# Causal mask products of the maxima stage, moved from 64x128 halves of TensorE's array to 64x64 quarters

## The chip, the cores and the metric

The kernel runs on one core of a Trainium2 chip. TensorE (PE), VectorE (DVE), ScalarE (ACT), GpSimd (POOL) and SyncE (SP) work beside each other, each through its own list of instructions in order; TensorE multiplies with an array of 128 rows by 128 columns and writes to the accumulation memory, PSUM. The metric is the device time of one execution in microseconds; profiled times of single instructions are in us or ns as marked.

## What is computed

The reference is a network of two layers on x of 2 x 1024 x 256. Each layer adds an attention and a feed-forward part, both computed from the same normalised x. The change is in layer 0's attention, which is causal, with 32 query heads and 8 key heads of 8 values each:

```python
scores = jnp.einsum('bhqd,bhkd->bhqk', q, k_rep) / scale
qpos = jnp.arange(T)[:, None]
kpos = jnp.arange(T)[None, :]
scores = jnp.where((kpos > qpos)[None, None], -jnp.inf, scores)
attn = jax.nn.softmax(scores, axis=-1)
out = jnp.einsum('bhqk,bhkd->bhqd', attn, v_rep)
```

Layer 0's feed-forward part works with values rounded to 8 bits; layer 1 has an attention without a mask and a feed-forward part with ternary weights.

## The kernel before

Layer 0's attention goes over 16 blocks of 128 queries: b is the batch, i the block in it, in the order (0, 0) to (0, 7) and then (1, 7) to (1, 0). Of each block the kernel first finds every row's maximum per head, and later computes the scores again, turned, with the maximum already taken off.

**The maxima.** `max_units` cuts a block into units, each a call of `max_unit`. A unit computes scores of 128 queries against some keys for a pair of head groups, e = 0 and 1. The values of e = 0 lie on rows 0 to 63 of the array and those of e = 1 on rows 64 to 127, so each score product (L958) uses 64 rows and all 128 columns, and the two halves write two PSUM buffers. Then VectorE reduces each buffer to the negated maxima (`tensor_reduce`, L970). The pool `ps_s` has three such buffers, of which a unit takes two. Blocks with i > 3 have 16 units over the first 512 keys without a mask. Every block has units over the keys that reach the diagonal, of width (i % 4 + 1) x 128: four heads to a unit with width 128, two with 256, one with 384 or 512.

**The mask** is added by TensorE, in `add_mask` (product at L930), because the last 128 keys of such a unit lie on the diagonal. `mask_q` holds, for query 64t + p of a block in row 64e + p, -1e30 at the keys after it and 0 elsewhere; `ident_h` holds the identity's rows 64t to 64t + 63, once in each half of the rows. Their product for t puts the mask onto the queries 64t to 64t + 63 and adds 0 to the other 64 queries. For t = 1 only the keys 64 to 127 are touched, as no query of the second half has a masked key before. One call is four products: t = 0 and 1, for e = 0 and 1. There are 208 calls and so 832 products: four per block of width 128 (before the scores, for four heads at once, 512 columns), sixteen per block of the other widths (after each score pair, 128 columns for t = 0 and 64 for t = 1). With width 256 a unit has two such calls.

**The weights and the rest.** `weigh` computes the turned scores: two pairs of products (L1022), one of 64 and one of 35 rows on each half, all 128 columns. ScalarE takes the exponential (L1032); GpSimd zeroes what is masked in blocks on the diagonal (L1036). `gather` multiplies by v: four products over 128 rows by 9 columns, each on its own column group, in two passes (L1052). `normalise` (L1067), `turn_rows` (L1083) and `output` (L1091) finish a block. Pieces of layer 0's feed-forward part (`gu`, L288, and `f0o`, L248, over the whole array), the normalisation and the weights of layer 1 stand between.

**The order.** TensorE's order is written by hand: `one_slot` runs one step, in which `advance` issues units of maxima as a credit allows, so that they spread over the steps of the blocks before; then comes a piece of other work, then the gathering and the weights of the block in hand. The other engines' order is set by the layer that records the program. The maxima of a block must be done before its weights start, by `LEAD` or `SHORT` steps.

Of the kernel before, what the change touches and what calls it, by code (L numbers as in the profile page):

```python
# [33 lines left out]
HALF = 64  # L34
# [14 lines left out]
def two_layers(ctx: ExitStack, tc: tile.TileContext, a: dict, out: bass.AP):  # L49
# [24 lines left out]
    for name, op, fill, sign in (  # L74
# [5 lines left out]
        for e in range(2):  # L80
            for t in range(2):
                part = m[HALF * e : HALF * e + HALF, t, :]
                nc.gpsimd.affine_select(
                    out=part,
# [7 lines left out]
    ident_h, mask_q = both.values()  # L92
# [645 lines left out]
    def attention0(w, qlast, tables):  # L738
# [11 lines left out]
        with ExitStack() as es:  # L750
# [171 lines left out]
            def add_mask(out, start, stop):  # L922


                for t in range(2):
                    lo = HALF * t
                    for e in range(2):
                        rows = slice(HALF * e, HALF * e + HALF)
                        rhs = mask_q[rows, t, None, lo:]
                        nc.tensor.matmul(  # L930
                            out[e][:, :, lo:],
                            ident_h[rows, t, :],
                            rhs.to_broadcast([HALF, out[e].shape[1], P - lo]),
                            start=start and t == 0,
                            stop=stop and t == 1,
                        )

            def wait_busy(n):
# [7 lines left out]
            def max_unit(b, i, pairs, lo, width, part, masked):  # L946
# [6 lines left out]
                if four:  # L953
                    add_mask([x.rearrange("p (h k) -> p h k", h=4) for x in sc], True, False)
                for s, p in enumerate(pairs):
                    for e in range(2):
                        rows = slice(HALF * e, HALF * e + HALF)
                        nc.tensor.matmul(  # L958
                            sc[e][:, s * width : (s + 1) * width],
                            qst[b, i][0][rows, p, :],  # L960
                            kst[b][0][rows, lo // 512, p // 4, 0:width],
                            start=not four,
                            stop=s == n - 1 if four else not masked,
                        )
                    if masked and not four:
                        end = (s + 1) * width
                        add_mask([x[:, None, end - P : end] for x in sc], False, True)
# [421 lines left out]
```

## Time and profile before

| what | value |
|---|---|
| time, median of 3 runs | 1179.34 us (1178.61 to 1179.58) |
| the profiled execution's own time | 1180.16 us |
| its span, first to last instruction | 1178.4 us |
| mean granted TensorE clock | 0.936 |
| L930 mask products | 832, 75.2 us busy, mean 221 ns |
| L930 weight loads | 832, 45.2 us busy, mean 97 ns |
| L970 reductions | 608, 372.8 us busy, mean 654 ns |
| L958 score products of the maxima | 768, 94.8 + 83.4 us busy |
| L1052 gathering | 1152 passes, 171.1 us busy |

Busy times of TensorE are unions of instructions that overlap: a product's duration holds its way through the array, so that the start of the next tells more of what it costs. PEld is the weight load, which runs beside PE. In a timeline, equal instructions that follow each other on an engine are merged into one row with a count; a bracket behind a row gives the idle time before it and what ended it. The chain of work that ended last is followed back from the last instruction: at each step to what released it, or to the instruction before it on its engine.

### The profile page before, as it was taken

How to read it: one execution, taken by the hardware profiler on the slowest of the kernel's cores; microseconds unless marked ns; L12 is line 12 of the kernel's file. 1: busy time of each engine (PE TensorE's matmuls, PEld its weight loads, DVE VectorE, ACT ScalarE, POOL GpSimd, SP SyncE). 2: the span in 40 equal slices, each digit the busy share in tenths (PEclk: the TensorE clock that was granted, in tenths of full speed). 3: DMA queues.
4: the chain of work that ended last, by engine and by line, in shares of the span. 5: the costliest groups of instructions: out<-in, count | busy, mean ns of one | idle time of the engine just before them, and what ended most of it. 6: DMA issues, size and time to landing. Idle time of an engine off the chain costs nothing.

```text
span 1178.4 us, 19285 instructions
## 1 busy us (share of the span) xinstructions
PE 1039.2 (88%) x7446; PEld 497.8 (42%) x7462; DVE 764.8 (65%) x1448; ACT 545.2 (46%) x983; POOL 345.4 (29%) x394
## 2 busy tenths in 40 slices
PE   5758787897988989897989998989999999999998
PEld 2333331231432222232323333334566676676676
DVE  7467988889688997789896899334333433433331
ACT  2004461673456757586767777742232322322221
POOL 2007233324235121412223335564222312312200
PEclk9758896998899989998999999999899999999989
DMA  5342101101102010100000110019431431421200
GB/s 173 112 110 73 48 3 38 21 21 45 49 5 50 1 27 10 41 5 8 21 19 10 27 28 3 5 19 132 62 52 28 80 65 30 86 51 28 38 19 19
DMA packets 65859, 48.99 MB, mean 42 GB/s; under 512 B 20840, under 2 KB 59368, under 8 KB 65768
## 3 DMA queue, kind: packets, MB, share of 16 engines
q1 hardware_dynamic: 60568, 39.05, 15.4%
q0 software_dynamic: 4112, 8.26, 2.9%
q8 instruction: 58, 0.95, 0.3%
q10 hardware_dynamic: 1088, 0.46, 0.1%
q14 instruction: 33, 0.27, 0.1%
HBM read 34.12 MB, written 15.20 MB: 42 GB/s over the span
## 4 chain that ended last, share of the span: by engine, by line
PE 55%; DVE 27%; DMA 7%; ACT 4%; POOL 3%; issue 2%; SPq 1%; DVEq 0%; ACTq 0%; POOLq 0%
DVE mx L970 14%; PE f1gu L632 8%; PE acc L1052 8%; PE s L1022 6%; PE f1o L667 5%; PE m L958 3%; PE sk L524 3%; PE sq L489 3%; PE gu L288 2%; DMA qscr<-ptq 2%; PE pqk L440 2%; ACT p L1032 2%; PE m L930 1%; DMA qkv<-all 1%; SPq L882 1%
## 5 line engine op out<-in xcount | busy, mean ns | idle before, releaser
L970 DVE TENSOR_REDUCE mx<-m 128x1 f32<-128x512 f32 (+3 forms) x608 | 372.8, 654 | 91.4 <-PE m L958 55.2
L1032 ACT ACTIVATE p<-s 128x512 f32<-128x512 f32 x576 | 307.0, 604 | 133.7 <-PE s L1022 131.2
L1052 PE MATMUL acc<-p,v 128*9 128x512 f32 x1152 | 171.1, 613 | 2.4 <-ACT p L1032 1.2
L958 PE MATMUL m<-k,qmain 64*128 64x512 bf16 (+3 forms) x384 | 94.8, 357 | 50.5 <-DVE mx L970 39.2
L1036 POOL TENSOR_SCALAR_AFFINE_SELECT p<-p 128x512 f32<-128x512 f32 x128 | 84.8, 685 | 162.2 <-ACT p L1032 161.9
L632 PE MATMUL f1gu<-xnT,wgu 128*128 128x512 f32 x256 | 117.6, 603 | 3.1 <-DVE wgu L1294 3.1
L958 PE MATMUL m<-kmain,qmain 64*128 64x512 bf16 (+3 forms) x384 | 83.4, 333 | 24.9 <-DVE mx L970 23.0
L958 PEld LDWEIGHTS <-qmain 64*128 64x128 bf16 x768 | 50.3, 99 | 80.4 <-issue 51.2
L930 PEld LDWEIGHTS <-ident_h 64*128 64x128 bf16 x832 | 45.2, 97 | 88.1 <-issue 65.3
L646 POOL TENSOR_TENSOR sq<-h 128x512 f32<-128x512 f32 x28 | 29.2, 1041 | 180.0 <-DVE h L642 180.0
L930 PE MATMUL m<-mask_q,ident_h 64*128 64x128 bf16 (+3 forms) x832 | 75.2, 221 | 2.4 <-DVE mx L970 2.3
L1022 PE MATMUL s<-qmain,k 64*128 64x512 bf16 x288 | 67.8, 393 | 9.0 <-ACT ob L258 3.1
L632 PEld LDWEIGHTS f1gu<-xnT,wgu 128*128 128x128 f32 x256 | 47.5, 195 | 51.8 <-issue 47.8
L1022 PE MATMUL s<-qmain,kmain 64*128 64x512 bf16 x288 | 64.0, 389 | 4.9 <-ACT p L1032 2.3
L1022 PE MATMUL s<-qlast,k 35*128 35x512 bf16 x288 | 64.0, 390 | 0.0
L641 DVE SCALAR_TENSOR_TENSOR h<-h,f1gu 128x512 f32<-128x512 f32 x32 | 22.0, 687 | 64.5 <-ACT h L640 64.5
L1022 PEld LDWEIGHTS <-k 64*128 64x128 bf16 (+1 forms) x576 | 21.1, 95 | 97.9 <-issue 89.8
L497 DVE TENSOR_REDUCE m<-sq 128x16 f32<-128x2048 f32 x16 | 36.7, 2292 | 39.6 <-PE sq L489 38.9
L1022 PE MATMUL s<-qlast,klast 35*128 35x512 bf16 x288 | 61.1, 386 | 0.0
L667 PE MATMUL f1o<-k,h 128*128 128x256 f32 x256 | 59.4, 388 | 0.5 <-DVE on L557 0.5
L667 PEld LDWEIGHTS f1o<-k,h 128*128 128x128 f32 x256 | 48.9, 193 | 9.0 <-issue 1.7
L640 ACT ACTIVATE h<-f1gu 128x512 f32<-128x512 f32 x32 | 19.1, 597 | 65.7 <-PE f1gu L632 65.6
(274 smaller groups left out, 1597.6 us busy)
## 6 DMA issues: line engine op xcount, KB each, us to landing
qmain<-qscr SPq DMA_DIRECT2D x64, 96.0 KB
qkv<-all SPq DMA_DIRECT2D x16, 384.0 KB
qscr<-ptq POOLq DMA_DIRECT2D x6, 384.0 KB, 4.1
x<-in_x SPq DMA_DIRECT2D x16, 128.0 KB
qmain<-qscr SPq DMA_DIRECT2D x32, 64.0 KB
qs<-qkv SPq DMA_DIRECT2D x16, 128.0 KB
ks<-qkv SPq DMA_DIRECT2D x16, 128.0 KB
vs<-qkv SPq DMA_DIRECT2D x16, 128.0 KB
```

The lines of the kernel that those rows point to most:

```text
L489: nc.tensor.matmul(ps[:, s, r, :], columns(q, slice(S * s, S * s + HD + 8), 4 * b + r), columns(k, slice(S * s, S * s + HD + 8), 4 * b + r ...
L497: nc.vector.tensor_reduce(m, ps, AX.X, ALU.max, negate=True)
L524: nc.tensor.matmul(ps[:, s, r, :], columns(k, slice(S * s, S * s + HD + 9), 4 * b + r), columns(q, slice(S * s, S * s + HD + 9), 4 * b + r ...
L632: nc.tensor.matmul(ps[g], wgu[:, k, g * HID + hc * P : g * HID + (hc + 1) * P], xnT[n][:, k, :], start=(k == 0), stop=(k == 1),)
L667: nc.tensor.matmul(po, hs[hc // 2][:, hc % 2, i * P : (i + 1) * P], wp[:, hc, :], start=(hc == 0), stop=(hc == NHC - 1),)
L930: nc.tensor.matmul(out[e][:, :, lo:], ident_h[rows, t, :], rhs.to_broadcast([HALF, out[e].shape[1], P - lo]), start=start and t == 0, stop ...
L958: nc.tensor.matmul(sc[e][:, s * width : (s + 1) * width], qst[b, i][0][rows, p, :], kst[b][0][rows, lo // 512, p // 4, 0:width], start=not ...
L970: reduced = nc.vector.tensor_reduce(mx[b, i][:, part, e, pairs[0] : pairs[0] + n], sc[e][:, : n * width].rearrange("p (s k) -> p s k", s=n ...
L1022: nc.tensor.matmul(sc[e], kst[b][n][rows, j // 4, u, j % 4 * P : (j % 4 + 1) * P], qst[b, i][n][rows, 4 * u : 4 * u + 4, :], start=n == 0, ...
L1032: nc.scalar.activation(p, sc[e], AF.Exp, scale=scale)
L1036: nc.gpsimd.affine_select(out=by_head, in_=by_head, compare_op=ALU.is_ge, fill=0.0, base=0, pattern=[[0, 4], [1, P]], channel_multiplier=-1,)
L1052: nc.tensor.matmul(acc[32 * s : 32 * s + HD0 + 1, :], vst[b][:, j, 4 * G + s, :], ps[s], start=(j == 0), stop=(j == i),)
```

## The change

Each of the four mask products now uses 64 columns of the array instead of 128: the product for t takes from `ident_h` only the columns of its own 64 queries and writes only those 64 partitions of PSUM. It no longer adds 0 to the other half of the queries. Where the masks come first in their buffer (width 128), the product for t = 1 now begins its own accumulation and covers all 128 keys of each head, 512 columns instead of 256, because nothing else has written its half before. Elsewhere the columns that stream, 128 and 64, are as before. The number of products and loads, their order on TensorE, and everything else in the source are the same; lines below move down by two.

```diff
             def add_mask(out, start, stop):
 
 
+
                 for t in range(2):
-                    lo = HALF * t
+                    lo = 0 if start else HALF * t
+                    queries = slice(HALF * t, HALF * t + HALF)
                     for e in range(2):
                         rows = slice(HALF * e, HALF * e + HALF)
                         rhs = mask_q[rows, t, None, lo:]
                         nc.tensor.matmul(
-                            out[e][:, :, lo:],
-                            ident_h[rows, t, :],
+                            out[e][queries, :, lo:],
+                            ident_h[rows, t, queries],
                             rhs.to_broadcast([HALF, out[e].shape[1], P - lo]),
-                            start=start and t == 0,
-                            stop=stop and t == 1,
+                            start=start,
+                            stop=stop,
                         )
```

## The prediction

> **What bounds the kernel now.** I read the page's busy shares first, then the waits between 79 and 746 us, the stretch in which nearly all mask products stand (rows run from 44.3 to 745.1 us; those before 79 us belong to blocks that wait for their query loads). Columns of the waits: us in total, times, longest.
>
> ```profile
> PE 1039.2 (88%) x7446; PEld 497.8 (42%) x7462; DVE 764.8 (65%) x1448; ACT 545.2 (46%) x983; POOL 345.4 (29%) x394
> ```
> ```profile
> PE m L958 <- DVE mx L970: 55.8, 88, 4.6
> ...
> DVE mx L970 <- PE m L958: 44.6, 40, 3.2
> DVE mx L970 <- PE m L930: 28.6, 36, 3.3
> ```
>
> Neither engine bounds this stretch alone. PE waits 55.8 us for VectorE to free a score buffer, and VectorE waits 44.6 + 28.6 us for PE to fill one. With three buffers and two to a unit, each holds the other up in turn. So I followed the chain of work that ended last through the stretch and asked, for each of the 208 calls of add_mask, on whose part of the chain it falls: 21 calls lie before 79 us, where the chain is loads; of the other 187, 99 lie on PE, 76 on VectorE (five of these are shared with idle issue time or ScalarE), 12 on ScalarE or GpSimd.
>
> **The price of one division of the array.** The timeline of PE gives it. Columns: start, duration, engine, line, operation, operands with rows*columns of the array, count. Durations contain some 0.16 us of pipeline, so I read from start to start.
>
> ```profile
> 203.07 0.39 PE L1022 MATMUL s<-qmain,k 64*128 64x512 bf16 x2
> 203.30 0.38 PE L1022 MATMUL s<-qlast,k 35*128 35x512 bf16 x2
> 203.52 0.38 PE L958 MATMUL m<-k,qmain 64*128 64x512 bf16 x2
> 203.83 1.04 PE L288 MATMUL gu<-xq,wg 128*128 128x512 bf16 x4
> 204.80 1.05 PE L1052 MATMUL acc<-p,v 128*9 128x512 f32 x8
> ```
>
> From 203.30 to 203.52 a pair of products of 512 columns takes 0.216 us (the two halves of the rows run beside each other; 512 columns at 2.4 per ns). From 203.52 to 203.83 the same pair takes 0.31 us, because a product over all 128 rows follows: 0.095 us in which nothing streams. The four gu products should take 4 x 0.216 = 0.864 us and take 0.97: again 0.1 us, and here the rows stay at 128 and only the columns change, from 128 to 9. Wherever the division changes at full clock, some 500 places, the loss is about 0.09 to 0.10 us; I take 0.095. The weight loads do not matter to it: it is the same before L1067, whose loads last 0.142 us, as before L1052 with 0.088.
>
> **What the change does to one call.** Now a call shares the division 64*128 with the score products around it:
>
> ```profile
> 583.29 0.27 PE L958 MATMUL m<-kmain,qmain 64*128 64x256 bf16 x2
> 583.40 0.25 PE L930 MATMUL m<-mask_q,ident_h 64*128 64x128 bf16 x4
> 583.48 0.27 PE L958 MATMUL m<-kmain,qmain 64*128 64x256 bf16 x2
> 583.59 0.25 PE L930 MATMUL m<-mask_q,ident_h 64*128 64x128 bf16 x4
> 583.77 1.50 PE L1052 MATMUL acc<-p,v 128*9 128x512 f32 x8
> ```
>
> The score pair of 256 columns takes 0.11, the call 0.08 (128 + 64 columns, one pair after the other), and where the gathering follows, 0.18, the loss included. After the change the four products lie on four quarters and should stream together: 128 columns, 0.055 us, so **0.027 us saved** per call. That four products on the same rows do stream together is seen in the gathering, whose four, on four column groups, start within 0.02 us of each other. In the 16 calls of width 128 the sum 512 + 256 columns becomes 512: 0.107 saved. Together 192 x 0.027 + 16 x 0.107 = 6.9 us.
>
> **What it adds** is a division on either side, 64*64, that nothing else uses. The order of PE's instructions is unchanged, so I can count: 207 of the 208 calls follow a score product in 64*128 and one follows products over the whole array, which change the division already. After the call, 67 go on with L958 and 47 with L1022, both 64*128, so that 114 need a second new change; the other 94 are followed by work that changes it anyway. 207 + 114 = 321 changes x 0.095 = **30.5 us**. Net on PE: 30.5 - 6.9 = 23.6 us, 0.113 us per call.
>
> No row shows a change to or from 64*64. Its bounds: below, nothing, if a change of columns alone were free; above, 0.1, the largest usual loss at full clock. I take the upper part, since 128*128 to 128*9, where the rows stay the same, costs it. A weight load of 64 columns isn't shown either; it lies between 0.088 (9 columns) and 0.094 us (L930's 128 columns), and I cost it at nothing, as the loss above is the same with every load. If that cover failed and one load per call were bare, it would be 208 x 0.09 = 19 us on PE. GpSimd's, ScalarE's and SP's instructions keep their order; VectorE's change in three places, each a small instruction (0.21 to 0.29 us) that changes place with a neighbour. I cost that at nothing, at most one reduction (0.68 us) each way.
>
> The Trainium skill has a rule on each side, and this paragraph can be left out. "TensorEngine Tiling (Array Packing)", Restrictions and Gotchas, says that column tiling excludes the fast weight load. In "TensorE: Matmul & The Clock Gate", LDWEIGHTS, a plain load takes columns / 1.2 ns, so by estimate 0.053 us for 64 columns. Were that bare once in every call, the sum would rise by 208 x 0.053 = 11 us. In the same page, Part 3, a pack of tiles takes one product plus some 4 ns per further tile and no change of division is priced; by that alone PE would gain the 6.9 us. The rows with 0.095 us speak against reading it so.
>
> **What of it is on the path.** The 99 calls on PE's part of the chain pay in full: 99 x 0.113 = 11.2 us. On VectorE's part another thing counts. Here PE has written the first half's scores and waits for a buffer for the second:
>
> ```profile
> 657.91 2.50 DVE L970 TENSOR_REDUCE mx<-m 128x1 f32<-128x512 f32 x4
> ...
> 658.65 0.37 PE L958 MATMUL m<-kmain,qmain 64*128 64x512 bf16 x1 [0.21 <-DVE mx L970]
> ...
> 658.65 0.45 PE L930 MATMUL m<-mask_q,ident_h 64*128 64x128 bf16 x4
> ```
>
> The four reductions take 2.50 us, 0.625 each, so the third, of this unit's first half, starts at about 659.16. The first half's masks start beside the late score product at 658.65 and are done at about 658.65 + 0.055 + 0.19 = 658.90: 0.26 us to spare. After the change the array must empty before it is divided anew, so both halves' masks come after the late product: 658.65 + 0.216 + 0.095 + 0.213 (a mask product's median duration) = 659.17, and with the 0.04 us from the end of a product to its reduction, VectorE stands still for 0.05. By the same sum: width 384, product 0.16, reductions 0.5 apart, 0.12; width 256, two calls to a unit, 0.25 for both, so 0.12 per call; width 128, 0.17. Weighted by the 64, 64, 48 and 12 calls of these kinds, about 0.10 us; 76 x 0.10 = **7.6 us**. The last 12 calls I cost at nothing: exponentials hide them, and without that cover they add 1.4 us. The 21 early calls are hidden by the query loads; without that, 2.4 us.
>
> Sum: 11.2 + 7.6 = 18.8 us. The profiled execution took 1180.16 us (span 1178.4), which gives 1199.0; the median shown, 1179.34, is 0.8 lower, so I predict **1198 us**. Late next will be PE: more of its products end VectorE's waits.
>
> **Rivals.** (1) *Columns may be divided freely.* If 64*128 and 64*64 need no emptying between them, only the savings stay: 6.9 us on PE, 3 to 6 of them on the path, 1173 to 1176 us, faster. It decides if the start of a score pair of 512 columns to the start of its masks stays at 0.22 us. For it: the rows stay divided at 64. Against it: 128*128 to 128*9 keeps its rows and loses 0.1. Chance 0.06.
>
> (2) *VectorE covers it.* PE's 55.8 us of waits are more than its 23.6 us of new work. Between one call and the next I find idle time on PE after 129 of the 208 calls; only the other 79 would then cost: 79 x 0.113 = 8.9 us less what later waits take back, 1180 to 1188 us. Against it: the head start of the first half is gone as well, so VectorE is late too. Chance 0.10, half of it within 0.2%.
>
> (3) *The quarters do not run together, or their loads are bare.* Two products over the same rows in turn give back the 6.9 us; bare loads add up to 19. With three quarters of these on the path, 1203 to 1217 us. Against it: the gathering's four starts and the steady 0.095. Chance 0.14.
>
> The forecast itself has 0.70, from 1188 (the chain's calls on PE, with a part taken back) to 1203 (all 23.6). A chain's count is a floor while PE grows more critical, which fits the upper half. More empty time can also bring further stretches at half clock; between 79 and 163 us the granted clock was 0.87 already.
>
> The range of 8 in 10 leaves out rival 1, the lower half of rival 2 and the top of rival 3: **1186 to 1210**. Faster by over 0.2% (about what a measurement can tell from no change): 0.06; within 0.2%: 0.05; slower: 0.89.
>
> **What would show it.** In the new profile, the start of a 512-column score pair to its mask call should go from 0.22 to 0.31 us, a call followed by score products from 0.08 to 0.15, and the four mask products should start together. The masks of a first half should no longer start beside a late score product. VectorE's waits for L930's successor should grow beyond 28.6 us, and all after 800 us should keep its length. I am wrong if the 0.22 stays, or if PE's waits for VectorE shrink by as much as PE's work grows.

## The result, and the profile after

The changed kernel takes 1196.12 us (median of 4 runs, 1192.43 to 1200.92), the kernel before 1179.46 beside it: 1.0137 times as long, 95% interval 1.0114 to 1.0161. That is 16.7 us more; the record said 1198, which is 18.8 more, in a range from 1186 to 1210. The profiled execution took 1196.97 us with a span of 1195.2, so it is 16.8 us above the one of before. An execution at a far lower granted clock (one of the kernel before, 1415.05 us at 0.64) stays out of every comparison.

The page of the kernel after: the shares of the engines, and the mask products and their weight loads, now at L932.

```profile
PE 1069.7 (89%) x7446; PEld 481.0 (40%) x7462; DVE 766.6 (64%) x1448; ACT 546.6 (46%) x983; POOL 344.1 (29%) x394
...
L932 PEld LDWEIGHTS <-ident_h 64*64 64x64 bf16 x832 | 24.7, 106 | 121.7 <-issue 118.4
```

PE is busy 30 us longer with the same 7446 products. VectorE, ScalarE and GpSimd are busy as before. A load of 64 columns lasts 106 ns on average, where 128 columns took 97.

The timeline of PE before, with two calls of width 256 that score products follow:

```profile
585.65 0.27 PE L958 MATMUL m<-kmain,qmain 64*128 64x256 bf16 x2
585.76 0.25 PE L930 MATMUL m<-mask_q,ident_h 64*128 64x128 bf16 x4
585.84 0.27 PE L958 MATMUL m<-kmain,qmain 64*128 64x256 bf16 x2
585.95 0.25 PE L930 MATMUL m<-mask_q,ident_h 64*128 64x128 bf16 x4
586.03 0.38 PE L1022 MATMUL s<-qmain,kmain 64*128 64x512 bf16 x2
```

And after, at the same kind of place:

```profile
591.28 0.38 PE L1024 MATMUL s<-qlast,klast 35*128 35x512 bf16 x2
591.50 0.27 PE L960 MATMUL m<-kmain,qmain 64*128 64x256 bf16 x2
591.71 0.24 PE L932 MATMUL m<-mask_q,ident_h 64*64 64x128 bf16 x4
591.88 0.28 PE L960 MATMUL m<-kmain,qmain 64*128 64x256 bf16 x2
592.10 0.24 PE L932 MATMUL m<-mask_q,ident_h 64*64 64x128 bf16 x4
592.27 0.39 PE L1024 MATMUL s<-qmain,kmain 64*128 64x512 bf16 x2
```

From the start of a score pair to its masks it was 0.11 us and is 0.20; from the masks to the next product it was 0.08 and is 0.18 (the record expected 0.15). Two calls, from 591.50 to 592.27, take 0.77 us with their score pairs; before, from 585.65 to 586.03, 0.39. All four products of a call start within 0.01 us of each other: four quarters do stream together. In width 128 the four of 512 columns also start together, and the scores follow 0.34 us later, where two in turn on each half of the rows would need 0.43 at least.

The same place in a unit where PE has waited for the second buffer:

```profile
599.33 0.27 PE L960 MATMUL m<-kmain,qmain 64*128 64x256 bf16 x1
600.37 0.27 PE L960 MATMUL m<-kmain,qmain 64*128 64x256 bf16 x1 [0.78 <-DVE mx L972]
600.57 0.24 PE L932 MATMUL m<-mask_q,ident_h 64*64 64x128 bf16 x4
```

Before, the first half's masks started in the same 0.01 us as the late score product (658.65 and 658.65). Now all four follow it by 0.20. The waits between 79 and 760 us (total, times, longest):

```profile
PE m L960 <- DVE mx L972: 52.1, 79, 4.6
DVE mx L972 <- PE m L960: 44.9, 41, 3.2
DVE mx L972 <- PE m L932: 40.2, 52, 3.4
```

VectorE's waits for the masks grew from 28.6 to 40.2 us. PE's for VectorE shrank by 3.7 only.

**Where the time came in.** Every unit ends in reductions, so the end of a block's last reduction cuts the trace into the blocks of maxima; (0, 4) to (1, 4) also have a part without masks. Added time against the kernel before, worked out from these ends in each profile, in us ("again" are second profiles of the same kernel):

| profile | blocks (0,0) to (0,2) | later parts with masks | parts without masks |
|---|---|---|---|
| after | 2.3 | 13.0 | 2.7 |
| after, again | 0.3 | 14.9 | 0.1 |
| repeated masks | 2.4 | 17.8 | 0.2 |
| repeated masks, again | 4.6 | 17.8 | 0.2 |
| padded weights | 5.6 | 11.5 | 0.0 |
| one-column quarter | 0.1 | 15.0 | 3.3 |
| one-column half (control) | 0.3 | 2.6 | -0.8 |
| merged calls | 0.0 | 11.9 | 0.9 |
| 64-row masks | -2.3 | -1.2 | 0.2 |
| no masks | 4.7 | -3.4 | -1.4 |

The control, whose time is that of before, shows how far such a sum can be off: 1.6 of its 2.6 us lie in the last block alone. All of the change's time lies in layer 0's attention and nearly all of it in parts that have masks; after the last gathering the kernel keeps its length (399.0 and 398.1 us against 400.2).

### The profile page after: what moved, and what is told of

It is laid out like the page before. It is cut to its first block, busy times and chain, and to the rows that moved or that the text cites. A ratio compares the mean times of both kernels' runs of the same rounds, so it can differ in the third digit from the quotient of the medians.

```text
span 1195.2 us, 19285 instructions
## 1 busy us (share of the span) xinstructions
PE 1069.7 (89%) x7446; PEld 481.0 (40%) x7462; DVE 766.6 (64%) x1448; ACT 546.6 (46%) x983; POOL 344.1 (29%) x394
## 4 chain that ended last, share of the span: by engine, by line
PE 63%; DVE 23%; DMA 4%; ACT 4%; POOL 3%; issue 2%; SPq 1%; DVEq 0%; ACTq 0%; POOLq 0%
DVE mx L972 12%; PE f1gu L632 9%; PE acc L1054 9%; PE s L1024 8%; PE f1o L667 5%; PE m L960 5%; PE sk L524 3%; PE sq L489 3%; PE gu L288 2%; PE pqk L440 2%; PE m L932 2%; DMA qscr<-ptq 2%; SPq L882 1%; PE acc L539 1%; ACT p L1034 1%
## 5 line engine op out<-in xcount | busy, mean ns | idle before, releaser
L960 PEld LDWEIGHTS <-qmain 64*128 64x128 bf16 x768 | 43.0, 98 | 86.5 <-issue 54.7
L932 PEld LDWEIGHTS <-ident_h 64*64 64x64 bf16 x832 | 24.7, 106 | 121.7 <-issue 118.4
L932 PE MATMUL m<-mask_q,ident_h 64*64 64x128 bf16 (+2 forms) x832 | 57.9, 248 | 1.2 <-DVE mx L972 1.2
```

The source lines that it names most:

```text
L932: nc.tensor.matmul(out[e][queries, :, lo:], ident_h[rows, t, queries], rhs.to_broadcast([HALF, out[e].shape[1], P - lo]), start=start, sto ...
L960: nc.tensor.matmul(sc[e][:, s * width : (s + 1) * width], qst[b, i][0][rows, p, :], kst[b][0][rows, lo // 512, p // 4, 0:width], start=not ...
```

## The experiments

**1. The length without the division.** The kernel before, with masks repeated in the old division:

```diff
-                for t in range(2):
+                order = (0, 1, 1) if start else (0, 0, 0, 1, 1)
+                for n, t in enumerate(order):
```

> The kernel before, with mask products repeated so that each call keeps PE as much longer as the change does, but in the old division of 64 rows by 128 columns: 320 more columns (0.135 us) in the 192 calls after the scores, 256 more (0.107 us) in the other 16, 27.6 us on PE in all. The repeated masks add -1e30 once more and change nothing. Theory (a change of division empties the array, which costs PE time and also the head start of a unit's first half): only the first part is here, so about half of 27.6 us, 1190 to 1194 us. Rival 'length alone' (nothing counts but PE's added time): as the change, 1195 to 1197. Rival 'loads' (bare loads of 64 columns cost, not the division): loads of 128 columns stay hidden, 1188 to 1194.

Measured: 1207.61 us (1201.81 to 1210.66), 1.0227 of before (1.019 to 1.0264). Beside the changed kernel on one chip, again:

> The run with repeated masks again, unaltered, beside the changed kernel. Its first four times lie between 1201.8 and 1210.7 us, its profile at the low end. If it stays 5 to 12 us above the changed kernel, then time in which the array streams inside the call costs more than as much time in which it empties; if both lie within 4 us, the difference was the chip's.

1204.22 us (1201.94 to 1206.6), 1.0208 (1.019 to 1.0225). All three theories expected less. By the timeline at full clock a padded call takes 0.139 us longer (0.108 in width 128), 28.4 us over all calls, and the changed kernel's net is the same (28.4, worked out below). The difference to the changed kernel, 8 us here, is not the chip's, but it is not the padding's alone either. The layer that orders the other engines moved GpSimd's work: the zeroing of the weights that a gathering waits for came before a piece of the key preparation (L775) and now comes behind it. First before, then with repeated masks:

```profile
106.09 1.22 POOL L1036 TENSOR_SCALAR_AFFINE_SELECT p<-p 128x512 f32<-128x512 f32 x2
107.28 2.16 POOL L775 TENSOR_TENSOR ptk<-restk,ptk 128x512 bf16<-128x512 f32 x1
```
```profile
103.30 1.16 POOL L775 TENSOR_TENSOR ptk<-restk,ptk 128x512 bf16<-128x512 f32 x1 [0.73 <-ACT ptk L774]
104.41 1.63 POOL L1037 TENSOR_SCALAR_AFFINE_SELECT p<-p 128x512 f32<-128x512 f32 x1
```

The gathering's weight loads waited for GpSimd between 79 and 130 us (total, times, longest) before, in the changed kernel, with repeated masks, and in two later runs with the same move, without masks (5) and with padded weights (7):

```profile
PEld acc L1052 <- POOL p L1036: 2.5, 3, 1.5
PEld acc L1054 <- POOL p L1038: 0.8, 2, 0.5
PEld acc L1053 <- POOL p L1037: 4.7, 2, 3.4
PEld acc L1047 <- POOL p L1031: 4.9, 2, 3.6
PEld acc L1066 <- POOL p L1050: 4.2, 2, 3.7
```

In these runs (the two of repeated masks, and the two later ones) block (0,2) alone takes 4.6 to 7.9 us longer than before; in the changed kernel and in the runs of 2, 3 and 4, where GpSimd and ScalarE keep their order in the blocks, at most 2.6. So only what comes from block (0,3) on can be compared with the change: 17.8 us in the parts with masks against 13.0 and 14.9, for as much time on PE. That time inside a call costs more when the array streams than when it empties is a reading of these parts and not shown, as VectorE's order differs in some places too.

> The changed kernel again, unaltered, beside the two length runs on one chip, for its spread: 1192 to 1201 us by the first four times.

The changed kernel gave 1196.28 us (1193.26 to 1197.91), 1.0137 (1.012 to 1.0154), the first result once more.

**2. A division and next to nothing else.** One product of one column, 64 by 64, ahead of the call's last, and as its control the same product over 128 columns:

```diff
+                        if t == 1 and e == 1:
+                            nc.tensor.matmul(
+                                out[1][HALF:, :, P - 1 :],
+                                ident_h[rows, 1, HALF:],
+                                mask_q[rows, 1, None, P - 1 :].to_broadcast([HALF, out[1].shape[1], 1]),
+                                start=False,
+                                stop=False,
+                            )
```

> The kernel before, with one more product per call ahead of the last one: a quarter, 64 by 64, of one column (four in width 128) that masks again a key that is masked or zero. It streams next to nothing and loads 64 columns once instead of four times, but asks for 2 changes of division in each of the 208 calls, 416 in all. Theory of the division: about 0.095 + 0.12 us and the shortest product, some 0.24 us per call, 50 us on PE, half or a little more of it on the path: 1204 to 1212 us, slower than the change itself. Rival 'loads': one bare load of 0.10 us per call, 21 us on PE, 1188 to 1193. Rival 'four products on quarters are slow': 1180 to 1184.

> Control of the one-column quarter: the same extra product at the same place, but of 64 rows by 128 columns, so without a change of division. Both theories: the shortest product, at most 0.03 us per call, 6 us on PE, 1179 to 1183 us.

The quarter: 1199.73 us (1198.08 to 1200.46), 1.0161 (1.0134 to 1.0189). The control: 1180.5, 1.0009 (0.9997 to 1.0022). So a product of 64 columns of weights that streams one column costs 20 us over 208 calls, and the same product in the old division nothing that can be measured. The timeline of the quarter's run (the one-column product is at L930, the call's others at L938):

```profile
592.03 0.24 PE L938 MATMUL m<-mask_q,ident_h 64*128 64x128 bf16 x3
592.21 0.19 PE L930 MATMUL m<-mask_q,ident_h 64*64 64x1 bf16 x1
592.33 0.20 PE L938 MATMUL m<-mask_q,ident_h 64*128 64x64 bf16 x1
592.46 1.04 PE L1060 MATMUL acc<-p,v 128*9 128x512 f32 x8
```

0.12 us pass from the one column to the next mask. The division is the cause, with the load of 64 columns that comes with it (no run has the one without the other), and rivals "loads" and "slow quarters" fall. But the sum fell short: the 416 changes gave 20 us, not the 25 to 33 that I expected. By the timeline at full clock a call takes 0.212 us longer, some 44 us on PE and not 50, and a smaller share of it reaches the total.

**3. Fewer changes.** The changed kernel, with the two calls of a unit of width 256 side by side:

```diff
-                    if masked and not four:
-                        end = (s + 1) * width
-                        add_mask([x[:, None, end - P : end] for x in sc], False, True)
+                for s in range(n if masked and not four else 0):
+                    end = (s + 1) * width
+                    add_mask([x[:, None, end - P : end] for x in sc], False, s == n - 1)
```

The second score pair also no longer starts an accumulation of its own.

> The changed kernel, but in units of width 256 both score pairs come first and then both mask calls, side by side: 64 changes of division fewer (257 instead of 321 new ones), the same products and loads. Theory of the division: 64 x 0.107 = 6.8 us less on PE, 3 to 5 us less than the change: 1191 to 1193 us. Rivals 'loads' and 'slow quarters': as the change, 1196 us.

1198.81 us (1194.56 to 1199.47), 1.015 (1.0122 to 1.0179): not faster by its times. Its profile shows the place clearly, though. In the three blocks of width 256 after the first rounds, (0,5), (1,5) and (1,1), the change adds 1.7, 1.5 and 1.6 us, the merged calls 0.3, 0.2 and 0.2. The profiled run took 1194.56 us at a granted clock of 0.930; the three others 1198.53 to 1199.47 at 0.924 to 0.927, and where they lost that has no trace. In those blocks the division's price goes when the division goes; whether the whole is faster is open.

**4. The saving without the division.** Both products read one triangle of 64 keys and use all 128 columns, so that 64 + 64 columns stream instead of 128 + 64:

```diff
-                    lo = HALF * t
+                    keys = slice(HALF * t, HALF * t + HALF)
...
-                        rhs = mask_q[rows, t, None, lo:]
+                        rhs = mask_q[rows, 0, None, 0:HALF]
...
-                            out[e][:, :, lo:],
+                            out[e][:, :, keys],
```

> The kernel before, with the same saving that the change aims at, but in the old division: both mask products read one triangle of 64 keys and carry it to their half of the keys through 128 columns of the array, product 0 onto the keys 0 to 63 (query q takes row q + 1), product 1 onto the keys 64 to 127 (queries 0 to 63 take row 0, in which all is masked, query 64 + j takes row j + 1). So 64 + 64 columns stream per call instead of 128 + 64, and in width 128, where the masks now come after the scores, 256 + 256 instead of 512 + 256. 192 x 0.027 + 16 x 0.107 = 6.9 us less on PE and no new change of division. Theory of the division: about half of it on the path, 2 to 5 us faster than before, 1175 to 1178 us. Rival 'PE's length counts in full': 1172 to 1174. Rival 'streaming in the masks is hidden': 1179 to 1181.

1182.34 us (1179.41 to 1185.14, 12 runs), 1.0008 of before (0.9996 to 1.0021): no difference. The profile tells where it went. The last gathering starts at 775.0 us instead of 778.2, so 3.2 us are saved there, within the 2 to 5 expected. But the rest, with the order of its instructions untouched, took 405.7 us instead of 400.2 (398.1 to 403.1 in the other profiles). The busy times in a stretch of the second layer, with the granted clock in the column after the engines, first before, then here:

```profile
930.00:1080.00 150.00, 148.52 (x1108) 104.46 (x1107) 55.30 (x89) 43.39 (x59) 34.43 (x30) 1.00 0.30 58
```
```profile
930.00:1080.00 150.00, 148.46 (x1093) 104.01 (x1090) 53.91 (x87) 41.52 (x58) 34.08 (x29) 0.98 0.28 56
```

The clock fell from 1.00 to 0.98; from the last gathering on, by the trace's clock records, 35.1 us pass at half clock instead of 27.0. It is one execution of each. The granted clock of all 12 runs is 0.932 on average, that of the kernel before beside them 0.935, which fits; that the 12 runs end where they do for this reason is not shown.

**5. No masks.** The kernel before without `add_mask`; the maxima also see the masked keys.

> The kernel before without add_mask: it leaves out the masks of the maxima, so that the maxima also see the keys after a query. 208 calls go, 192 x 0.083 + 16 x 0.32 = 21 us less on PE, and VectorE may start on a unit that much sooner. Slope on the other side of the same quantity. Theory (about half of PE's time in the calls is on the path): 8 to 13 us less, 1167 to 1172 us. Rival 'length in full': 1157 to 1160.

1181.37 us (1175.3 to 1186.08), 0.9993 (0.9972 to 1.0014). Taking 21 us from PE left the time where it was, which no theory expected. The table tells in which parts: from block (0,3) on, 4.8 us are gained (3.4 in the parts with masks), a quarter of the 18.9 us that those blocks lost on PE; in the first three blocks 4.7 us are added, with 7.1 in (0,2), where GpSimd's zeroing comes late, as shown under 1. So this run is no clean slope. The granted clock fell as well, between 80 and 130 us from 0.90 (first row, before) to 0.84 (second, without masks):

```profile
80.00:130.00 50.00, 39.01 (x232) 16.52 (x232) 36.29 (x74) 18.79 (x34) 25.67 (x27) 0.90 0.33 93
```
```profile
80.00:130.00 50.00, 36.55 (x137) 11.60 (x136) 29.85 (x55) 15.80 (x28) 25.01 (x25) 0.84 0.32 90
```

From 79 us to the last gathering, by the clock records, 112.5 us pass at half clock, against 89.4 before, 105.4 and 98.1 in the two profiles of the changed kernel and 86.2 and 88.7 with repeated masks. All ten runs have a granted clock of 0.924 to 0.933, the kernel before beside them 0.925 to 0.942. What the clock took back and what GpSimd's order did are not separated; that less work alone lengthens the time at half clock is not shown either, since with the 6.9 us less of run 4 it is 87.1 us.

**6. Four score buffers.** `ps_s` with four buffers and `ps_t` with three, in both kernels:

```diff
-            ps_s = es.enter_context(tc.tile_pool(name="a0s", bufs=3, space=PSUM))
-            ps_t = es.enter_context(tc.tile_pool(name="a0t", bufs=4, space=PSUM))
+            ps_s = es.enter_context(tc.tile_pool(name="a0s", bufs=4, space=PSUM))
+            ps_t = es.enter_context(tc.tile_pool(name="a0t", bufs=3, space=PSUM))
```

> The kernel before with four score buffers for the maxima instead of three, and three instead of four for the rest. Two whole units fit, so PE does not wait in the middle of a unit and the head start of a first half is of little use. What the lost buffer costs elsewhere is not known: 1165 to 1200 us. It is the base of the next run.

> The changed kernel with the same four and three buffers. Theory of the record (7.6 of the 18.8 us are the lost head start): 9 to 13 us slower than the kernel before with four buffers. Rival 'PE's time alone, the head start costs nothing': 15 to 20 us slower than it, like the change itself.

1201.57 us (1.0163, 1.0131 to 1.0196) and 1209.08 (1.0238, 1.0194 to 1.0282). The change costs 7.5 us here by the medians and 8.9 by the two ratios (their difference, 0.0075, is uncertain by about 0.005, so some 2 to 15 us), not 16.7: below both expectations by its middle, and nearer to the first. PE's waits for VectorE are half as long with four buffers, here in the kernel before:

```profile
DVE mx L970 <- PE m L958: 54.1, 38, 3.2
DVE mx L970 <- PE m L930: 46.9, 54, 3.8
PE m L958 <- DVE mx L970: 26.4, 45, 4.8
```

This fits a price that passes through the shared buffers. It is no proof: the base itself takes 20 us more than the kernel before, the other engines' order changed with it, and the lost `ps_t` buffer gave PE other waits, in which added work can hide too.

**7. The same length elsewhere.** As in 1, but the extra columns are computed into the buffers of the next step of weights:

> The kernel before with the same 27.6 us more on PE as the run with repeated masks (320 columns per call, 256 in width 128, old division), but not inside the mask call: the extra products are computed into the score buffers of the next step of weights, where the step's own scores overwrite them. So a unit's reductions are not put off by their own call, only by the time that PE lost before. Theory 'what puts off the reductions is what costs' : well below the run with repeated masks, 1188 to 1196 us. Rival 'PE's length counts in full, wherever it lies': as that run, 1201 to 1210 us.

1201.28 us (1199.08 to 1208.04), 1.0197 (1.0173 to 1.0222): the rival's low end, not mine. But the profile (1199.08 us) divides it: from block (0,3) on, this padding adds 11.5 us in the parts with masks, the padding inside the call 17.8; in the first three blocks it adds 5.6, where GpSimd's order changed as under 1. So the whole time decides nothing between the two. The granted clock between 80 and 130 us was 0.82 there, against 0.90 before, but the changed kernel's was 0.81 and its first three blocks took only 2.3 us more.

## Why the prediction was right, point by point

**The price of a division: right.** From the end of a score pair's columns to the masks 0.089 to 0.093 us passed (0.095 forecast), though no row of before had a 64 by 64 division. The number of changes is as counted: up to the last gathering 820 instead of 499, so 321 more.

**The weight loads, costed at nothing: a small miss.** I took the loss as the same with every load. Leaving the quarters takes 0.117 to 0.120 us, not 0.095, whatever follows. After the change of division a mask's load starts within 0.002 us of its product (591.705 and 591.706); before, it started 0.11 us ahead (585.649 and 585.759). A mask product of 128 columns lasts 0.240 us in place of 0.213, and one of 64 columns 0.213 in place of 0.187: 0.026 more each, about what 64 columns take to pass (0.027). I read that as one load of 64 columns per call that is partly bare, 0.023 us by the timeline, 208 x 0.023 = 4.8 us on PE. The record had named one bare load per call as a bound, at 0.09; it is a quarter of that. PE's net is then 23.6 + 4.8 = 28.4 us instead of 23.6.

**The saving: right.** Four quarters stream together, so 6.9 us of columns are gone.

**The head start: seen, its price not separated.** All four masks now wait for the late score product, and VectorE's waits for masks grew by 11.6 us. Its size in the sum, 7.6 us of 18.8, was not shown. The runs bear on it from three sides, read in the parts with masks from block (0,3) on, per us that the timeline shows added to PE there (187 of the 208 calls, so 187/208 of 30.0 us for the padded weights, at 0.146 us per call, of 44.2, 28.4 and 28.4): the padding of the weights 11.5 / 27.0 = 0.43 and the one-column quarter 15.0 / 39.7 = 0.38, neither of which holds up a first half in its own call; the change 13.0 to 14.9 / 25.5, 0.51 to 0.58; repeated masks, which hold up both halves by their whole length, 17.8 / 25.5 = 0.70. That order fits: what puts off a reduction costs more than what only keeps PE longer. But the control's 2.6 us would move each of these by about 0.1, and in whole times the two paddings differ little (1.0197 and 1.0208, with overlapping intervals), so this stays a reading of profiles.

**The 99 calls on PE's part of the chain: plausible, not shown apart.** 99 of 187 is 0.53, between the lowest and highest of these shares, so the count that was meant as a floor may be near the whole. The total came out 2 us below the forecast, with a larger net on PE and a smaller share of it on the path: with 28.4 us on PE the record's own sum would have given 99 x 0.137 + 7.6 = 21.1 us, and 16.7 were measured. So the mechanism was right, and that the total came so close is in part luck: the bare load, which I left out, and a share on the path that was too dear partly cancel.

**The order of the other engines: right.** GpSimd, ScalarE and SyncE do their work in the same order after the change, and VectorE's order differs in three places, as the record said. It matters more than I knew: where an experiment moved GpSimd's work, one block took 4.6 us and more.

**The rivals.** Free columns (1) would have kept 0.11 and 0.08 in the timeline: no. VectorE's cover (2) would have shrunk PE's waits by what PE gained in work: they shrank by 3.7 us. Serial quarters (3): no; its bare load: yes, small.

**The clock** was named only as a risk. The change's two profiles spend 9 and 16 us more at half clock in the attention stage than before; in the first of them, 3.3 us of the added time lie in parts (0,6) and (0,7) without masks, and the second has none of that. What these stretches cost is not separated.

The Trainium skill's page "TensorEngine Tiling (Array Packing)", Key Properties, says that a change of tiling mode drains TensorE. Here that is 0.09 us on entry. Its Restrictions name the loss of the fast load with column tiling; here a load of 64 columns took 0.103 us (median) where 128 took 0.094, which fits, but no run here shows which kind of load either was. The estimate of the record from "TensorE: Matmul & The Clock Gate", 0.053 bare per call, was too high: the timeline shows 0.023.

**Still open:** whether time in which the array empties costs less per us than time in which it streams, once the other engines keep their order; what the head start is worth; why the time at half clock grew without the masks; where the length runs spend the extra time of their longer executions, of which there is no trace; and whether the merged calls are faster than the change.

## What to carry to other kernels

Before cutting products into smaller tiles of the array, look at the division of the products on either side, count how often it would change, and price a change from start to start in the trace: a call with 0.027 us to save cannot pay for two changes of 0.09 us. If the columns saved are real, seek a form that keeps the neighbours' division, as the 64-row masks do; here that saved 3.2 us in its stage, and the whole time showed no gain. And when an experiment adds work to an engine or takes it away, compare the order of the other engines before the times: here padding and leaving out masks on TensorE also moved GpSimd's work, and one block took 4.6 to 7.9 us longer.

## What the runs showed of the hardware that was not expected

With 21 us of products less on TensorE, the time at half clock in the stage was 112.5 us instead of 89.4, and the whole time stayed within 0.3%; GpSimd's order had changed too, so the cause is open. A weight load of half the columns was slower than a full one (0.103 against 0.094 us). The two row halves of the array start out of their written order when one of them waits (before: a first half's second mask at 400.49 us, the other half's first mask, written ahead of it, at 400.63), and where the masks begin with a change of division all four start together, behind the late product (600.57).
